# The third recurrent step of a gated graph network with its gates by nodes instead of by channels

## The chip, the cores and the metric

The kernel runs on one core of one Trainium2 chip. The metric is the device time of one execution in microseconds (us). The kernel before took 2534.15 us, the median of 3 runs (2533.99 to 2534.88).

A core has five engines, each with an instruction queue that it works through in order: TensorE (PE in the profile; its weight loads are listed as PEld), VectorE (DVE), ScalarE (ACT), GpSimd (POOL) and SyncE (SP), which here only issues transfers. They meet through semaphores. TensorE writes to PSUM, in banks of 128 partitions by 512 fp32 values; the other tiles of the kernel lie in SBUF.

## The reference, cut to what matters

64 graphs of 256 nodes with 256 channels, fp32, and an adjacency matrix of integers for each. Layer 0 is a gated graph network of three steps with shared gate weights, layer 1 a graph attention with four heads. Both have a normalization ahead and a residual around them.

```python
def _gru_cell(inp, h, w_ih, w_hh, b_ih, b_hh):
    gi = inp @ w_ih.T + b_ih
    gh = h @ w_hh.T + b_hh
    i_r, i_z, i_n = jnp.split(gi, 3, axis=-1)
    h_r, h_z, h_n = jnp.split(gh, 3, axis=-1)
    r = jax.nn.sigmoid(i_r + h_r)
    z = jax.nn.sigmoid(i_z + h_z)
    n = jnp.tanh(i_n + r * h_n)
    return (1.0 - z) * n + z * h

# layer 0
h = jnp.maximum(_layernorm(x), 0.0)
h0 = h
A = (adj != 0).astype(x.dtype)
for i in range(3):
    m = jnp.einsum('bnd,de->bne', h0, weight[i])
    aggr = jnp.einsum('bst,bsd->btd', A, m)
    h0 = _gru_cell(aggr, h0, w_ih, w_hh, b_ih, b_hh)
x = x + h0
# layer 1
h = jnp.maximum(_layernorm(x), 0.0)
x = x + gat(h, adj, W, b, a)      # four heads, masked softmax over the neighbours
```

## The kernel before, in words

Two graphs ("sequences" 0 and 1) make a pair; 32 pairs run one after the other, overlapped. Everything is planned in ticks: `at(tick, phase, p, fn)` puts a piece of work into a plan, and at the end the plan is emitted tick by tick, within a tick first the phase STEP, then READY, then REST, and within a phase the later pair first. That order of emission is the order on every engine's queue. A step of the recurrence takes six ticks (`SUB = 6`), the pairs start 18 ticks apart (`APART`), and pair p has its three steps at ticks 0 to 5, 12 to 17 and 24 to 29 of its own count. So exactly one step is in STEP at any time: the first step of pair p+1, the third of pair p, the second of pair p+1, and so on. Between them, in READY and REST, lie the normalizations, transposes, attention and transfers of the pairs around.

In all three steps the channels lie on the partitions: state hT, sums aggr, gates R and Z and the new value hn are tiles of 128 partitions by 2 channel halves by 512 (2 sequences of 256 nodes). `block` (L308, its matmuls at L312) makes one 256x256 product for one sequence: four matmuls with a 128x128 piece of a weight loaded and 256 nodes of the data moving. An fp32 matmul is two instructions in the profile, so a block is eight. `part` (L418) is one matmul with a 128x128 weight loaded; the three-products scheme for the state's share of the n gate has seven of them in a step: N00, NS1, NS2, N01, NS3, NS4, N11. They go into the banks qa and qb. Blocks are named by weights: RH, S1, S2, RA (gate r), RZ, S4, ZA (r of sequence 1, z), and NA once per sequence (input of gate n, banks pn0 and pn1).

The gate banks come from a ring of five (`ps_g`), the others from a ring of three (`ps_m`).

`tick_0` runs N00, copies qa to qb on ScalarE (L433), aggregates over the neighbours (L440, the copies to SBUF at L444), runs NS1 and copies m5n (L446). `tick_1` runs NS2; VectorE adds `q_b[:, N:] = q_b[:, :N] + m5n` (L453); block RH into pc; N01; ScalarE takes hn with its bias (`state_n`, L421) and copies pc to pd (L459); VectorE forms T3 and T2 (L461, L462). `tick_2` runs NS3 into `q_b[:, :N]`, which L453 has read, and NS4 into `q_b[:, N:]`, the last hn on VectorE (L468), block S1 with its copy m5 (L473), and T4 (L474). `tick_3` has S2 into pd, the sum into pe on VectorE (L479), RA and the first tanh (`tanh_half`, L425). `tick_4`: N11, `first_n(0)` ((R+1)·hn into pn0 on VectorE, L495), RZ, the sum for Z (L489), S4, tanh. `tick_5`: `first_n(1)`, NA of sequence 0 on top of pn0, ZA, NA of sequence 1, and `new_n` (tanh on ScalarE, L506, then the difference h − n on GpSimd, L510) for each. The biases are columns, one value per partition, and go in as the bias operand of ScalarE's activations, one instruction per channel half.

In READY of the tick behind a step, `update` (L527, L528 on VectorE) makes the new hT for both sequences. One and two ticks behind, `back` turns hT to nodes on partitions with four transposes per sequence (`turn_back`, L770): after steps one and two it takes from them the halves hNhi and hNlo for the next aggregation (L760, L761), after step three it adds them to x (`residual`, L776). x then goes through the second normalization (L339 to L351) and on to the attention. `divided` (L551, L553, L558) belongs to the attention's output of an earlier pair: VectorE divides a product (`po`, L542), GpSimd adds it to x. `maxima` (L899), the leaky relu (L919), the masks (L872) and the exponentials (L934) are also the attention's, each at ticks of its own.

The last pair's end is written out by hand in `plan_tail`: a tuple of pieces in the order in which they are emitted, sequence 0 ahead of sequence 1, with the leftover attention of the two pairs before in between.

Of the kernel before, what the change touches and what calls it, by code (L numbers as in the profile page):

```python
# [26 lines left out]
def gated_gnn_then_gat_kernel(  # L27
# [69 lines left out]
    def bank(name):  # L97
# [3 lines left out]
        "x": 5, "adj": 2, "edge": 2, "noedge": 2, "hT_a": 2, "xn": 2, "val": 2, "row": 4, "zz": 4, "o": 2,  # L101
# [44 lines left out]
    w_msgs += [load_square("row", f"w_msg_{l}", weight[l]) for l in range(1, L)]  # L146
# [39 lines left out]
    bhn = const.tile([P, KD], F32, name="bhn")  # L186

# [120 lines left out]
    def block(pt, w, j, src, start=False):  # L308

        for c in range(KD):  # L310
            for k in range(KD):
                nc.tensor.matmul(  # L312
                    pt[:, ts(c, N)], w[:, k, j * D + c * P : j * D + (c + 1) * P], src[:, k, :],
                    start=start and c == 0 and k == 0, stop=(c == KD - 1 and k == KD - 1),
                    skip_group_check=True,
                )

# [66 lines left out]
    class Step:  # L384


        def __init__(self, n_, l, hT, end):

            self.n_, self.l, self.hT, self.end = n_, l, hT, end
# [25 lines left out]


# [5 lines left out]

        def tanh_half(self, i, dst, src, g0):
            for c in range(KD):
                nc.scalar.activation(  # L425
                    of(dst, i)[:, c, :], src[:, c, :], AF.Tanh, bias=brz[:, g0 + c : g0 + c + 1], scale=0.5
                )

# [19 lines left out]
        def tick_1(self):  # L448
            h0 = of(self.hT(), 0)
            q_a, q_b = self.qa, self.qb  # L450
            self.own("hn", [P, KD, T])
            self.part(q_b[:, :N], NS2, self.T2n)
            nc.vector.tensor_add(q_b[:, N:], q_b[:, :N], self.m5n)  # L453
            p_c = self.bank("pc")
            block(p_c, w_h, RH, h0, start=True)
            self.part(q_a[:, :N], N01, h0[:, 1, :])
            self.state_n(0, 0, q_a[:, :N])
            self.bank("p5")
            nc.scalar.copy(self.bank("pd"), p_c)  # L459
            T3 = self.own("T3", [P, KD, N])  # L460
            nc.vector.tensor_sub(T3, of(self.aggr, 1), of(self.hT(), 1))  # L461
            nc.vector.tensor_add(self.own("T2", [P, KD, N]), T3, h0)  # L462

        def tick_2(self):
            q_b = self.qb
            self.part(q_b[:, :N], NS3, self.T3n)
            self.part(q_b[:, N:], NS4, of(self.hT(), 1)[:, 1, :])
            nc.vector.scalar_tensor_tensor(  # L468
                of(self.hn, 1)[:, 1, :], q_b[:, :N], bhn[:, 1:2], self.m5n, op0=ALU.add, op1=ALU.add
            )  # L470
            self.state_n(0, 1, q_b[:, N:])
            block(self.p5, w_a[self.l], S1, self.T1, start=True)
            nc.scalar.copy(self.own("m5", [P, T]), self.p5)  # L473
            nc.vector.tensor_sub(self.own("T4", [P, KD, N]), self.T2, of(self.aggr, 0))  # L474

        def tick_3(self):
            R_ = self.own("R", [P, KD, T])
            block(self.pd, w_a[self.l], S2, self.T2)
            nc.vector.tensor_add(self.bank("pe"), self.pd, self.m5)  # L479
            block(self.pc, w_a[self.l], RA, of(self.aggr, 0))  # L480
            self.tanh_half(0, R_, by_c(self.pc), 0)

        def tick_4(self):
            Z_ = self.own("Z", [P, KD, T])
            self.part(self.qb[:, :N], N11, self.T4n)
            self.state_n(1, 0, self.qb[:, :N])
            self.first_n(0)
            block(self.pd, w_h, RZ, self.T3)
            nc.vector.tensor_add(of(Z_, 1), by_c(self.pd), by_c(self.m5))  # L489
            block(self.pe, w_a[self.l], S4, of(self.aggr, 1))  # L490
            self.tanh_half(1, self.R, by_c(self.pe), 0)
# [7 lines left out]
        def input_n(self, i):  # L499
            block(getattr(self, f"pn{i}"), w_a[self.l], NA, of(self.aggr, i))  # L500

        def new_n(self, i):
            n__ = of(self.hn, i)
            p_n = by_c(getattr(self, f"pn{i}"))
            for c in range(KD):
                nc.scalar.activation(  # L506
                    n__[:, c, :], p_n[:, c, :], AF.Tanh, bias=bi[:, 2 * KD + c : 2 * KD + c + 1]
                )
            if not (self.end and i == 1):
                nc.gpsimd.tensor_sub(of(self.R, i), of(self.hT(), i), n__)  # L510

        def tick_5(self):
            self.first_n(1)
            self.input_n(0)
            self.tanh_half(1, self.Z, of(self.Z, 1), KD)
            block(self.pd, w_a[self.l], ZA, self.T4)
            self.new_n(0)
            self.tanh_half(0, self.Z, by_c(self.pd), KD)
            self.input_n(1)
            self.new_n(1)  # L520

        def update(self, i):

            d_ = of(self.R, i)
            if self.end and i == 1:
                nc.vector.tensor_sub(d_, of(self.hT(), i), of(self.hn, i))
            nc.vector.scalar_tensor_tensor(d_, of(self.Z, i), 1.0, d_, op0=ALU.add, op1=ALU.mult)  # L527
            nc.vector.scalar_tensor_tensor(of(self.hT(), i), d_, 0.5, of(self.hn, i), op0=ALU.mult, op1=ALU.add)  # L528

# [33 lines left out]
    def plan_tail(t0, p, v, g, turn_back, residual):  # L563


        val, zz, own, drow, mrow = None, {}, {}, {}, {}
# [22 lines left out]
        def result(i):  # L589
            if i == 0:  # L590
# [99 lines left out]
        def do(what, q, *key):  # L690
# [3 lines left out]
        order = (  # L694
            lambda: g.update(0), do("rows", 1), do("product", 2, 0), lambda: turn_back(0), lambda: g.update(1),
            do("product", 2, 1), lambda: residual(0), lambda: stats(0), do("add", 1), lambda: turn_back(1),
            do("product", 2, 2), lambda: residual(1), lambda: result(0), lambda: turned(0), lambda: stats(1),
            do("product", 2, 3), do("divided", 2, 0), lambda: values(0), lambda: result(1), lambda: turned(1),
            do("divided", 2, 1), do("divided", 2, 2), lambda: values_out(0), do("divided", 2, 3),
            do("write", 2), lambda: spread_scores(0), lambda: logits(0), lambda: leaky(0),  # L700
            lambda: values(1), lambda: values_out(1), lambda: maxima(0), do("exps", 1, 0), lambda: spread_scores(1),
            lambda: logits(1), lambda: leaky(1), lambda: spread_tops(0), do("product", 1, 0), do("product", 1, 1),
            lambda: maxima(1), lambda: spread_tops(1), do("exps", 1, 1), do("divided", 1, 0), do("divided", 1, 1),
            lambda: exps(0), do("product", 1, 2), do("product", 1, 3), lambda: exps(1), do("divided", 1, 2),
            do("divided", 1, 3), do("write", 1), lambda: output(0), lambda: output(1),
        )
        for k, fn in enumerate(order):
            at(t0 + SUB * (2 * L - 1) + 0.01 * (k + 1), READY, p, fn)

    def plan_pair(p):  # L710
# [40 lines left out]
        def back(l, i):  # L751

            def fn():
                if l < L - 1 and i == 0:
                    v["hN"] = node_halves(f"{p}_{l}")
                turn_back(l, i)
                pt = v["pback", i]
                hi, lo = (flat(y[:, i * KN : (i + 1) * KN, :]) for y in v["hN"])
                if l < L - 1:
                    nc.scalar.copy(hi, pt)  # L760
                    nc.vector.tensor_sub(lo, pt, hi)  # L761
                else:
                    residual(i)
            return fn

        def turn_back(l, i):
            pt = v["pback", i] = bank(f"pback_{p}_{l}_{i}")
            for s in range(KN):
                for k in range(KD):
                    nc.tensor.transpose(  # L770
                        pt[:, s * D + k * P : s * D + (k + 1) * P], h["hT"][:, k, ts(i * KN + s, P)], ident
                    )

        def residual(i):
            xi = flat(v["x"][:, i * KN : (i + 1) * KN, :])
            nc.vector.tensor_add(xi, v["pback", i], xi)  # L776

        for l in range(L):
            end = last and l == L - 1
            g = Step(f"{p}_{l}", l, lambda: h["hT"], end)  # L780
            t = 2 * SUB * l
            ready(t - 3 if l else t - 1, g.state_sums)
            ready(t + 2, g.last_state_sum)
            step(t, lambda g=g: g.tick_0(v["hN"], v["edge"]))
            for k, fn in enumerate((g.tick_1, g.tick_2, g.tick_3, g.tick_4, g.tick_5), 1):
                step(t + k, fn)
            if not end:
                ready(t + SUB, lambda g=g: g.update(0))
                ready(t + SUB, lambda g=g: g.update(1))
                for i in range(PB):  # L790
# [16 lines left out]
        if last:  # L807
            plan_tail(t0, p, v, g, lambda i: turn_back(L - 1, i), residual)
# [169 lines left out]
    at(2, REST, 0, load_vectors)  # L978
    at(5, REST, 0, lambda: step_weights_T(1))
# [38 lines left out]
```

## Time and profile before

| | |
|---|---|
| median of 3 runs | 2534.15 us |
| the profiled execution | 2540.86 us |
| its span, first to last instruction | 2539.1 us |
| mean granted TensorE clock | 0.995 |
| one period of the steady part (one pair) | 76.95 us |
| L312, blocks on TensorE, 6912 instructions | 13 to 20% of the chain of waits for each of pd, pn, pc |
| L418, parts on TensorE, 1344 instructions | 379 to 391 ns listed, by group |
| L770, transposes back, 768 instructions | 116.1 us busy |
| L776, residual additions on VectorE, 64 | 43.9 us busy, 685 ns each |
| L510, differences on GpSimd, 191 | 317.8 us busy, 1664 ns each |

The page lists for each engine the time in which at least one instruction was under way. TensorE's matmuls overlap, so a listed duration is longer than the distance from one start to the next; distances are read from the timeline. VectorE's and ScalarE's instructions overlap by less. A number in brackets behind a timeline line is the time that the engine stood idle before that instruction and what ended it.

### The profile page before, as it was taken

The page shows a single profiled execution, that of the slowest core. Times are in us where ns is not written, and L with a number is a line of the kernel's source. Part 1 is how long each engine was busy: PE and PEld are TensorE (multiplying, and loading weights), DVE is VectorE, ACT ScalarE, POOL GpSimd, SP SyncE. Part 2 cuts the span into 40 slices and gives each one's busy share as a digit, 9 for nine tenths or more (in the row PEclk, how much of TensorE's full clock was granted, in tenths as well). Part 3 has the DMA queues.
Part 4 walks back from the last instruction along what each step waited for, and adds up shares of the span by engine and source line. Part 5 has one row for each costly group of instructions (what it writes and reads, how often), then busy time and mean ns, then how long its engine had stood idle before and what let it go on. Part 6 is the DMA issues. An engine that isn't in the chain of part 4 may idle for free.

```text
span 2539.1 us, 38539 instructions
## 1 busy us (share of the span) xinstructions
PE 2514.5 (99%) x13918; PEld 2246.4 (88%) x13918; DVE 1824.1 (72%) x4458; ACT 1466.2 (58%) x3095; POOL 645.5 (25%) x514
## 2 busy tenths in 40 slices
PE   8999999999999999999999999999999999999998
PEld 6888898888889888989888988888988889898887
DVE  5567777677777777776777776777777777767667
ACT  3456565565555565555665655655656656556664
POOL 0122232222222222323232323222222223222221
PEclk9999999999999999999999999999999999999998
DMA  3033434553435544345544444534344544354443
GB/s 94 17 74 88 97 93 108 109 125 92 92 92 117 109 113 99 87 95 117 117 100 93 98 102 109 125 92 100 88 113 109 119 95 93 87 124 110 93 95 89
DMA packets 168223, 251.91 MB, mean 99 GB/s; under 512 B 42896, under 2 KB 128352, under 8 KB 168032
## 3 DMA queue, kind: packets, MB, share of 16 engines
q0 software_dynamic: 33728, 130.03, 26.6%
q1 hardware_dynamic: 132736, 119.41, 16.0%
q8 instruction: 110, 1.80, 0.3%
q14 instruction: 81, 0.66, 0.1%
q10 hardware_dynamic: 1568, 0.01, 0.0%
HBM read 215.62 MB, written 25.67 MB: 95 GB/s over the span
## 4 chain that ended last, share of the span: by engine, by line
PE 97%; DVE 1%; DMA 1%; ACT 1%; issue 0%; POOL 0%; SPq 0%; DVEq 0%
PE pd L312 20%; PE pn L312 13%; PE pc L312 13%; PE po L542 9%; PE pa L440 7%; PE qb L418 6%; PE pe L312 6%; PE p L312 6%; PE qa L418 5%; PE pv L820 4%; PE pback L770 3%; PE pt_a L370 1%; PE pt_b L370 1%; PE pc L238 1%; DVE any L899 0%; DMA hh_nat<-in_L_gnn_w_hh_dram 0%
## 5 line engine op out<-in xcount | busy, mean ns | idle before, releaser
L510 POOL TENSOR_TENSOR R<-hT_a,hn 128x512 f32<-128x512 f32 x191 | 317.8, 1664 | 879.4 <-ACT hn L506 821.5
L312 PE MATMUL pn<-aggr,w_a 128*128 128x256 f32 x1536 | 367.1, 382 | 0.0
L312 PE MATMUL pd<-T,w_a 128*128 128x256 f32 x1536 | 366.3, 381 | 0.0
L312 PEld LDWEIGHTS pn<-aggr,w_a 128*128 128x128 f32 x1536 | 287.0, 190 | 43.1 <-DVE pn L495 6.4
L312 PEld LDWEIGHTS pd<-T,w_a 128*128 128x128 f32 x1536 | 287.9, 191 | 37.6
L542 PEld LDWEIGHTS po<-val,zz 128*128 128x128 f32 x2048 | 250.3, 195 | 4.5
L542 PE MATMUL po<-val,zz 128*128 128x65 f32 x2048 | 247.2, 275 | 0.0
L899 DVE CUSTOM_DVE_ANT_0 any<-drow,noedge 128x256 f32<-128x256 f32 x496 | 236.9, 478 | 9.8 <-DMA drow<-score_dram 1.0
L506 ACT ACTIVATE hn<-pn,bi 128x256 f32<-128x256 f32 x384 | 160.3, 469 | 144.3 <-PE pn L312 144.2
L425 ACT ACTIVATE R<-pc,brz 128x256 f32<-128x256 f32 x192 | 80.5, 470 | 278.5 <-PE pc L312 278.5
L527 DVE SCALAR_TENSOR_TENSOR R<-Z,R 128x512 f32<-128x512 f32 x192 | 131.8, 687 | 147.6 <-POOL R L510 142.8
L558 POOL TENSOR_TENSOR x<-x,o 128x256 f32<-128x256 f32 x124 | 112.0, 904 | 481.6 <-DVE o L553 481.6
L761 DVE TENSOR_TENSOR hNlo<-pback,hNhi 128x512 fp32r<-128x512 f32 x128 | 88.4, 691 | 201.6 <-ACT hNhi L760 201.6
L919 ACT ACTIVATE zz<-zz,val 128x256 f32<-128x256 f32 x496 | 224.9, 509 | 0.0
L495 DVE SCALAR_TENSOR_TENSOR pn<-R,hn 128x512 f32<-128x512 f32 x192 | 142.5, 742 | 93.7 <-ACT hn L421 77.2
L425 ACT ACTIVATE R<-pe,brz 128x256 f32<-128x256 f32 x192 | 80.5, 470 | 185.9 <-PE pe L312 185.9
L528 DVE SCALAR_TENSOR_TENSOR hT_a<-R,hn 128x512 f32<-128x512 f32 x192 | 174.6, 909 | 14.3 <-ACT m5n L446 1.4
L312 PE MATMUL pd<-T,w_h 128*128 128x256 f32 x768 | 181.5, 379 | 0.0
L312 PE MATMUL pc<-aggr,w_a 128*128 128x256 f32 x768 | 181.5, 379 | 0.0
L312 PE MATMUL pe<-aggr,w_a 128*128 128x256 f32 x768 | 181.4, 379 | 0.0
L312 PE MATMUL pc<-hT_a,w_h 128*128 128x256 f32 x768 | 181.4, 379 | 0.0
L312 PE MATMUL p<-T,w_a 128*128 128x256 f32 x768 | 181.4, 379 | 0.0
(176 smaller groups left out, 5258.5 us busy)
## 6 DMA issues: line engine op xcount, KB each, us to landing
zz<-score_dram POOLq DMA_DIRECT2D x62, 1024.0 KB, 11.7
zz<-topT_dram POOLq DMA_DIRECT2D x62, 1024.0 KB, 8.7
adj<-in_adj_dram SPq DMA_DIRECT2D x64, 512.0 KB
drow<-score_dram SPq DMA_DIRECT2D x62, 512.0 KB
x<-in_x_dram SPq DMA_DIRECT2D x32, 512.0 KB
out_dram<-x SPq DMA_DIRECT2D x31, 512.0 KB
noedge_dram<-noedge SPq DMA_DIRECT2D x31, 256.0 KB
score_dram<-score SPq DMA_DIRECT2D x124, 4.0 KB
```

What stands on the lines that cost most here:

```text
L312: nc.tensor.matmul(pt[:, ts(c, N)], w[:, k, j * D + c * P : j * D + (c + 1) * P], src[:, k, :], start=start and c == 0 and k == 0, stop=(c ...
L418: nc.tensor.matmul(pt, w_n[:, j, :], src, start=start, stop=True, skip_group_check=True)
L425: nc.scalar.activation(of(dst, i)[:, c, :], src[:, c, :], AF.Tanh, bias=brz[:, g0 + c : g0 + c + 1], scale=0.5)
L440: nc.tensor.matmul(pt[:, ts(i, N)], hN[half][:, i * KN + s, ts(e, P)], edge[:, i * KN + s, :], start=(s == 0 and half == 0), stop=(s == KN ...
L495: nc.vector.scalar_tensor_tensor(by_c(self.bank(f"pn{i}")), of(self.R, i), 1.0, of(self.hn, i), op0=ALU.add, op1=ALU.mult)
L506: nc.scalar.activation(n__[:, c, :], p_n[:, c, :], AF.Tanh, bias=bi[:, 2 * KD + c : 2 * KD + c + 1])
L510: nc.gpsimd.tensor_sub(of(self.R, i), of(self.hT(), i), n__)
L527: nc.vector.scalar_tensor_tensor(d_, of(self.Z, i), 1.0, d_, op0=ALU.add, op1=ALU.mult)
L528: nc.vector.scalar_tensor_tensor(of(self.hT(), i), d_, 0.5, of(self.hn, i), op0=ALU.mult, op1=ALU.add)
L542: nc.tensor.matmul(po[:, ts(h_, VC)], zz[:, j, h_, ts(s, P)], v["val"][:, i * KN + j, ts(h_, VC)], start=(j == 0), stop=(j == KN - 1),)
L899: nc.vector.tensor_tensor_reduce(any_, drow[r // KN][:, h, :], v["noedge"][:, r, :], 1.0, -3.0e38, ALU.add, ALU.max, accum_out=v["top"][:, ...
L919: nc.scalar.activation(zz[:, h, :], zz[:, h, :], AF.Prelu, alpha=ALPHA, bias=v["val"][:, r, S0 + H + h : S0 + H + h + 1],)
```

## The change

Steps one and two of each pair stay as they are. The third step becomes a class of its own, `LastStep`, with nodes on the partitions for its gates: `block` and `part` load 128x128 pieces of the data and move the weights (256 columns in `block`, 128 in `part`). R, Z, hn and the new value come out by nodes, so the four transposes per sequence behind the step are gone, and `update` adds straight into x. As the biases now run along the free dimension, they are kept as rows that are the same on all partitions (`b_rows`, six row loads and four VectorE operations once); they are added on VectorE, or copied by ScalarE into a bank before the matmuls add to it. The update needs the state after step two by nodes: `back` of step two keeps a copy `h` of it.

```diff
-        "x": 5, "adj": 2, "edge": 2, "noedge": 2, "hT_a": 2, "xn": 2, "val": 2, "row": 4, "zz": 4, "o": 2,
+        "x": 5, "adj": 2, "edge": 2, "noedge": 2, "hT_a": 2, "xn": 2, "val": 2, "row": 2, "zz": 4, "o": 2,
...
-    w_msgs += [load_square("row", f"w_msg_{l}", weight[l]) for l in range(1, L)]
+    w_msgs += [load_square("noedge", f"w_msg_{l}", weight[l]) for l in range(1, L)]
...
+    def load_bias_rows():
+        for j, vector, g in ((BR, b_ih, 0), (BZ, b_ih, 1), (BI, b_ih, 2), (BH, b_hh, 2)):
+            nc.sync.dma_start(b_rows[:, j, :], on_all_rows(vector, g))
+        others = []
+        for g in range(2):
+            others.append(buf("o", [P, D], f"b_hh_{g}"))
+            nc.sync.dma_start(others[g], on_all_rows(b_hh, g))
+        at(9, READY, 0, lambda: bias_rows(others))
...
+    class LastStep(Step):
...
+        def block(self, pt, w, j, src, start=False):
+            for s in range(KN):
+                for k in range(KD):
+                    nc.tensor.matmul(
+                        pt[:, ts(s, D)], src[:, k, ts(s, P)], w[:, k, ts(j, D)],
+                        start=start and s == 0 and k == 0, stop=(s == KN - 1 and k == KD - 1),
+                        skip_group_check=True,
+                    )
+
+        def part(self, pt, j, src, start=False):
+            for s in range(KN):
+                nc.tensor.matmul(
+                    pt[:, ts(s, P)], src[:, ts(s, P)], w_n[:, j, :], start=start and s == 0, stop=True,
+                    skip_group_check=True,
+                )
...
+        def state_n(self, c, i, pt):
+            nc.vector.tensor_add(
+                self.mine(self.hn, i)[:, :, ts(c, P)], pt.rearrange("q (s n) -> q s n", s=KN), self.row(BH, c)
+            )
+
+        def last_state_n(self):
+            by_s = self.m5n.rearrange("q (s n) -> q s n", s=KN)
+            nc.vector.tensor_add(by_s, by_s, self.row(BH, 1))
+            nc.vector.tensor_add(
+                self.mine(self.hn, 1)[:, :, ts(1, P)], self.qb[:, :N].rearrange("q (s n) -> q s n", s=KN), by_s
+            )
+
+        def tanh_half(self, i, dst, src, g0):
+            nc.scalar.activation(self.mine(dst, i), src, AF.Tanh, scale=0.5)
+
+        def first_term(self):
+            return self.pc, False
+
+        def tick_0(self, hN, edge):
+            super().tick_0(hN, edge)
+            nc.scalar.copy(by_c(self.bank("pc")), self.row(BR))
...
+        def new_n(self, i, h):
+            hn_ = self.mine(self.hn, i)
+            p_n = by_c(getattr(self, f"pn{i}"))
+            nc.vector.tensor_add(p_n, p_n, hn_)
+            nc.scalar.activation(hn_, p_n, AF.Tanh)
+            if not (self.end and i == 1):
+                nc.gpsimd.tensor_sub(self.mine(self.R, i), self.nodes(h, i), hn_)
...
+        def tick_4(self):
...
+            self.first_n(0)
+            for i in range(PB):
+                nc.scalar.copy(by_c(self.bank(f"pn{i}")), self.row(BI))
+            self.block(self.pd, w_h, RZ, self.T3)
+            nc.vector.tensor_add(by_c(self.pd), by_c(self.pd), self.row(BZ))
+            nc.vector.tensor_add(self.mine(Z_, 1), by_c(self.pd), by_c(self.m5))
...
+        def tick_5(self, h):
+            self.first_n(1)
+            self.input_n(0)
+            self.input_n(1)
+            self.tanh_half(1, self.Z, self.mine(self.Z, 1), KD)
+            self.block(self.pd, w_a[self.l], ZA, self.T4)
+            self.new_n(0, h)
+
+        def tick_5_rest(self, h):
+            self.new_n(1, h)
+            self.tanh_half(0, self.Z, by_c(self.pd), KD)
+
+        def update(self, i, h, x_):
+            d_, n__, xi = self.mine(self.R, i), self.mine(self.hn, i), self.nodes(x_, i)
+            if self.end and i == 1:
+                nc.vector.tensor_sub(d_, self.nodes(h, i), n__)
+            nc.vector.tensor_add(xi, xi, n__)
+            nc.vector.scalar_tensor_tensor(d_, self.mine(self.Z, i), 1.0, d_, op0=ALU.add, op1=ALU.mult)
+            nc.vector.scalar_tensor_tensor(xi, d_, 0.5, xi, op0=ALU.mult, op1=ALU.add)
...
 # in back, behind step two
+                if l == L - 2:
+                    nc.scalar.copy(flat(v["h"][:, i * KN : (i + 1) * KN, :]), pt)
...
+            if final:
+                step(t + 5, lambda g=g: g.tick_5(v["h"]))
+                rest(t + 5, lambda g=g: g.tick_5_rest(v["h"]))
```

`tick_5_rest` stands in REST of its tick, behind the READY work; `update` stays in READY of the tick behind the step, now with an addition of x ahead of its two operations. In the last pair's hand-written order, sequence 1 now goes ahead of sequence 0, and the two `turn_back` and two `residual` pieces are gone.

## The prediction

> **What bounds the kernel now.** I read the page's busy shares and its chain of waits first, then the waits, then the timeline of the one period in which the changed step and the step behind it run, engine by engine.
>
> ```profile
> PE 2514.5 (99%) x13918; PEld 2246.4 (88%) x13918; DVE 1824.1 (72%) x4458; ACT 1466.2 (58%) x3095; POOL 645.5 (25%) x514
> ...
> PE 97%; DVE 1%; DMA 1%; ACT 1%; issue 0%; POOL 0%; SPq 0%; DVEq 0%
> ```
>
> TensorE sets the end. In the steady part the timeline repeats every 76.95 us (an aggregation starts at 1200.43, its successor at 1277.38), and 32 pairs of 76.95 make 2462 of the 2539.1 us span. TensorE hardly waits: the only wait on its path that recurs is 0.2 us of a weight load, 30 times. So a TensorE instruction removed is worth its spacing, and any new wait of TensorE costs all of it. The spacing is not the listed duration, since matmuls overlap: blocks of eight 256-column instructions start 1.73 us apart, 0.216 us each.
>
> The place that matters lies one tick behind the changed step, where the next pair's second step starts. These are the weight loads, VectorE and GpSimd of that place (start, duration, what it is):
>
> ```profile
> 1281.50 0.41 PEld L418 LDWEIGHTS qa<-hT_a,w_n 128*128 128x128 f32 x2
> 1281.93 0.57 PEld L770 LDWEIGHTS pback<-ident,hT_a 128*128 128x128 f32 x4
> 1282.47 0.30 PEld L418 LDWEIGHTS qb<-T3n,w_n 128*128 128x128 f32 x2
> ```
>
> ```profile
> 1276.93 0.18 DVE L551 RECIPROCAL rden<-po 128x4 f32<-128x4 f32 x1 [2.20 <-PE po L542]
> 1277.21 0.42 DVE L553 TENSOR_TENSOR o<-po,rden 128x256 f32<-128x256 f32 x1
> 1277.56 0.68 DVE L527 SCALAR_TENSOR_TENSOR R<-Z,R 128x512 f32<-128x512 f32 x1
> 1277.72 1.12 POOL L558 TENSOR_TENSOR x<-x,o 128x256 f32<-128x256 f32 x1 [0.34 <-DVE o L553]
> 1278.27 1.12 DVE L528 SCALAR_TENSOR_TENSOR hT_a<-R,hn 128x512 f32<-128x512 f32 x1
> 1279.31 0.68 DVE L527 SCALAR_TENSOR_TENSOR R<-Z,R 128x512 f32<-128x512 f32 x1
> 1280.09 0.69 DVE L528 SCALAR_TENSOR_TENSOR hT_a<-R,hn 128x512 f32<-128x512 f32 x1
> 1280.70 0.42 DVE L899 CUSTOM_DVE_ANT_0 any<-drow,noedge 128x256 f32<-128x256 f32 x1
> ...
> 1281.52 0.43 DVE L453 TENSOR_TENSOR qb<-qb,m5n 128x256 f32<-128x256 f32 x1
> ```
>
> VectorE stands still until a product of TensorE ends (1276.93), then runs without a gap to L453. The NS3 part of TensorE adds into what L453 reads, so it may not start before L453 ends at 1281.95; its load starts at 1282.47. The slack is 0.52 us, and 0.44 us of it is the four transposes in between (matmul starts 1282.14 to 1282.58), which the change removes.
>
> The second place is the changed step's own first tick: ScalarE and the load of block RH.
>
> ```profile
> 1250.39 1.07 ACT L444 COPY aggr<-pa 128x512 f32<-128x512 f32 x2
> 1251.34 0.40 ACT L446 COPY m5n<-qa 128x256 f32<-128x256 f32 x1
> 1251.60 1.09 ACT L934 ACTIVATE zz<-zz 128x1024 f32<-128x1024 f32 x1
> ```
>
> ```profile
> 1251.28 1.49 PEld L312 LDWEIGHTS pc<-hT_a,w_h 128*128 128x128 f32 x7
> ```
>
> RH is ready to start while ScalarE is still behind with the sums' copies.
>
> **The change, per pair.** *Transposes removed:* eight per pair, two fours of 0.44 us: −0.88.
>
> *Blocks:* still eight instructions of 256 columns; 0.
>
> *Parts:* seven per step, each now four instructions of 128 columns instead of two of 256. Before: two by 0.216 = 0.432. The nearest row is the spread of scores near the end, 128x128 against 128 columns: sixteen in 1.95 us, less the last one's 0.28, over 15, is 0.111 each, so 0.446 a part and +0.10 for seven. Bounds: 0.108, the transposes' spacing, gives 0; the other spread (2.02 us for sixteen) gives 0.116 and +0.24.
>
> *Bias row in pc:* RH no longer clears its bank but adds to a ScalarE copy of the bias row, put behind the copy of m5n. That copy can start at 1251.60, where the exponential starts now; the 128x512 copy of L459 takes 0.59, so 1252.19. RH's load wants to start at 1251.28, some 0.03 later by the longer parts: a wait of 0.91. Not all is lost: at 2456.07 the loads had waited 0.98 and the matmuls, due at 2455.25 (two of 0.227 behind 2454.80), 0.82; in shorter waits about 0.1 comes back too. I take +0.82; bounds 0.65 and 0.95. The exponentials queued behind the copy have two ticks of room.
>
> *Residual into update:* the two additions of L776 (0.685 each, in the ticks behind) go, two additions x+n of SBUF tiles (0.68, issued 0.60 apart like the neighbours here) come, but ahead of L453: +1.20 on that chain, against 0.08 of slack left.
>
> *Later input of the last difference:* VectorE now adds hn to pn before each tanh. The first addition waits for block NA of sequence 0, which ends near 1271.65, so first_n(1), this addition, the four normalizations (1.37) and two maxima (0.92) end near 1274.6, and GpSimd's first difference, in the midst of them, adds some 0.95 as it does now (the second maximum takes 1.37 instead of 0.42). The second addition then ends near 1276.3, its tanh near 1276.95, and GpSimd's second difference, 1.27 long, runs from 1277.0 to 1278.3, where now it is over at 1277.38. The first x+n, due at 1277.56, meets it. That neither runs through the other is read from L528 above: 1.12 instead of 0.69 beside a GpSimd addition. So +0.75 more on the chain.
>
> Sum for NS3: 1.20 + 0.75 − 0.08 + 0.05 to wake = 1.9 of wait; by the 0.1 to 0.2 that comes back, +1.75. Bounds: without the collision, and with the 0.43 that L528 loses now gone, 0.60; with GpSimd's next addition losing its turn into L527 too, 2.4. I take 1.75, since the first difference delays the maxima today and will again.
>
> The Trainium skill's "SBUF — State Buffer", section "Who interferes with whom", calls the port pair of VectorE and GpSimd an exclusive lock, which blocks a VectorE instruction with two SBUF inputs for the whole of a GpSimd instruction that reads SBUF. By it x+n would wait for the whole rest of the difference, 0.75; by the L528 row alone, which lost 0.43 beside a shorter operation, the pair would cost 0.3 less.
>
> *At nothing, with the cover:* ScalarE loses three hn copies, runs six whole tanhs for twelve halves, and gains three bias copies and two of h (0.58); those of h fall into its idle stretches of 2.04 and 3.68 us before the hn copy at 1233.05 and the tanh at 1239.23; uncovered they would be 1.2. VectorE waits for N01 in the changed step, with T3 and T2 queued behind; T2 then ends near 1256.2 and block S2 loads at 1259.5 even with RH late. Its three state additions and the split L468 (1.7) come before the addition into pe, which has RA, a product and N11 (3.9) to spare. The two additions on pd (1.38) end near 1268.4; ZA comes after both NA blocks at 1273.2. The bias copies into pn wait for the hn addition at 1265.8; NA needs them at 1269.8. TensorE waits at none of these; each is worth its overrun if VectorE is 2 us later than I count.
>
> *Once:* six row loads and their six SP issues (about 0.4 each, as L119) at tick 3, where the transfer queues are nearly empty; four VectorE operations (1.6) at tick 9, needed at tick 24. Two fewer "row" buffers: a pair's destination scores are fetched eight ticks behind the last maximum of the pair before. 0 to 2 us in all; I take 0.
>
> *The last pair:* its eight transposes ran in two groups at half clock (0.86 each between 2487.34 and 2492.36): −1.7, with +0.10 and +0.82: −0.8. The end can shift by some 4 us either way, since that half clock may come or go with the gap before it.
>
> **Sum.** −0.88 + 0.10 + 0.82 + 1.75 = +1.79 per pair, by 31 = +55.5, less 0.8: +54.7. On the profiled span of 2539.1 (2540.86 around it) that is 2593.8; the median of the runs lies 6.7 below the profiled execution, so 2534.15 + 54.7 = **2588.9**.
>
> **Rivals.** *(A) The forecast*, 50%: with 1.3 to 2.2 for NS3, 2575 to 2603. *(B) Only the added instructions delay L453*, 25%: the second difference is out of the way before 1277.5, NS3 costs 0.60 to 1.05, per pair +0.64 to +1.09: 2553 to 2567. For it: GpSimd is idle 75%. Against: the 1.37 us maximum. *(C) Only RH waits*, 5%: +0.04 per pair: 2535, no change; it needs L453 not to decide, against the 0.08 of slack. *(D) Faster*, 10%: the transposes come out whole and neither wait appears, −0.78 by 31 − 0.8: 2509. The mechanism is TensorE's 99% share; it decides if ScalarE's and VectorE's lateness together stay under 0.78 a pair. Against it: both line-by-line orders. *(E) The clock drops*, 10%: TensorE ran at half clock in two stretches:
>
> ```profile
> 94.00:96.00 2.00, 2.00 (x7) 1.63 (x7) 0.17 (x1) 0.00 (x0) 0.00 (x0) 0.53 0.00 0
> ...
> 2488.00:2496.00 8.00, 8.00 (x40) 8.00 (x39) 5.79 (x18) 2.97 (x8) 3.57 (x4) 0.50 0.29 58
> ```
>
> The granted clock (behind the five engines) fell after 1.94 us of idle within 4 us, and after 1.5 us at 2483.7. The first spell lasted some 3.4 us. A new wait of 1.9 us could do it each period: 1.7 more per pair, up to 2589 + 53 = 2642. Against: a 1.25 us gap at 53 did nothing. The Trainium skill's "TensorE: Matmul & The Clock Gate", section "Why this matters for your kernels", would put the limit at gaps of about 3 us; by it E never happens, by the 1.5 us row it can, and the row decides.
>
> Anything below 0.2% (5 us) I call no change. Faster 0.10 (D), same 0.05 (C), slower 0.85 (A, B, E). The range reaches from B's low end to a part of E: 2550 to 2620; A's own is 2575 to 2603.
>
> **What would show it.** In each period two waits of TensorE: RH for ScalarE's copy into pc (near 0.9) and the next step's NS3 for L453 (near 1.9, 0.7 under B); period 78.7 instead of 76.95; parts of four at 0.111; GpSimd's second difference overlapping the first x+n. Wrong would be: parts spaced above 0.13 (weight loads as the bound), no wait at RH, or a wait in a place that I put at nothing.

## The result, and the profile after

| | before | after |
|---|---|---|
| median of 4 runs each | 2534.52 us | 2594.69 us (2593.44 to 2595.51) |
| ratio to before, 95% interval | | 1.0235 (1.0218 to 1.0253) |
| span of the profiled execution | 2539.1 us | 2591.5 us |
| period of the steady part | 76.95 us | 78.65 us |
| TensorE busy | 2514.5 us, 99% | 2506.4 us, 97% |

The changed kernel is slower by 2.35%. The period grew by 1.70 us, and 31 of these are 52.7 us, where the spans differ by 52.4. The page's busy shares, then the shares of its chain of waits:

```profile
PE 2506.4 (97%) x14110; PEld 2236.1 (86%) x14110; DVE 1932.8 (75%) x4686; ACT 1463.8 (56%) x2967; POOL 636.0 (25%) x514
...
PE 84%; DVE 9%; ACT 5%; issue 2%; DMA 0%; DVEq 0%; POOL 0%; SPq 0%
```

TensorE's listed busy time falls by 8 us, as transposes went (by less than their spacing, since a part of each new wait lies inside listed durations); yet it holds only 84% of the chain instead of 97%, and VectorE and ScalarE have taken the rest. The waits of the weight loads say where (who waited for whom: us in total, times, longest):

```profile
PEld qb L446 <- DVE qb L490: 53.3, 31, 2.1
PEld pc L574 <- ACT pc L611: 25.3, 32, 0.8
PEld pn L437 <- DVE pn L530: 6.2, 29, 0.2
```

The third row is the wait that was there before. The first two are new and come once a pair: 1.72 us for L490 (L453 before), 0.79 us for the copy of the bias row. What a wait cost is read beside it, from where the matmuls start against where their spacing would have put them. The first place, the changed step's first tick, in the timelines of ScalarE, of the loads and of TensorE:

```profile
1198.83 0.40 ACT L483 COPY m5n<-qa 128x256 f32<-128x256 f32 x1
1199.09 0.62 ACT L611 COPY pc<-b_rows 128x512 f32<-128x512 f32 x1
```

```profile
1198.45 0.53 PEld L582 LDWEIGHTS qb<-w_n,T2n 128*128 128x128 f32 x4
1199.77 1.59 PEld L574 LDWEIGHTS pc<-w_h,hT_a 128*128 128x128 f32 x8 [0.79 <-ACT pc L611]
```

```profile
1198.56 0.61 PE L582 MATMUL qb<-w_n,T2n 128*128 128x128 f32 x4
1199.77 1.99 PE L574 MATMUL pc<-w_h,hT_a 128*128 128x256 f32 x8 [0.60 <-ACT pc L611]
1201.60 0.61 PE L582 MATMUL qa<-w_n,hT_a 128*128 128x128 f32 x4
...
1202.48 0.61 PE L582 MATMUL qb<-w_n,T3n 128*128 128x128 f32 x4
1202.93 0.61 PE L582 MATMUL qb<-w_n,hT_a 128*128 128x128 f32 x4
```

NS2 started at 1198.56; four instructions of 0.111 and RH's eight of 0.216 put N01 at 1200.73. It started at 1201.60: 0.87 lost. The last two rows are parts back to back, 0.45 apart (0.444 from the whole row of starts).

The second place, one tick behind the changed step: the loads, then GpSimd and VectorE:

```profile
1229.94 0.41 PEld L446 LDWEIGHTS qa<-hT_a,w_n 128*128 128x128 f32 x2
1232.10 0.30 PEld L446 LDWEIGHTS qb<-T3n,w_n 128*128 128x128 f32 x2 [1.75 <-DVE qb L490]
```

```profile
1225.24 1.29 POOL L623 TENSOR_TENSOR R<-h,hn 128x512 f32<-128x512 f32 x1 [2.28 <-ACT hn L621]
1226.49 1.19 POOL L690 TENSOR_TENSOR x<-x,o 128x256 f32<-128x256 f32 x1
```

```profile
1225.37 0.18 DVE L683 RECIPROCAL rden<-po 128x4 f32<-128x4 f32 x1 [0.83 <-PE po L674]
1225.66 0.42 DVE L685 TENSOR_TENSOR o<-po,rden 128x256 f32<-128x256 f32 x1
1226.00 1.09 DVE L658 TENSOR_TENSOR x<-x,hn 128x512 f32<-128x512 f32 x1
1227.01 1.22 DVE L659 SCALAR_TENSOR_TENSOR R<-Z,R 128x512 f32<-128x512 f32 x1
1228.26 0.69 DVE L660 SCALAR_TENSOR_TENSOR x<-R,x 128x512 f32<-128x512 f32 x1
1228.87 0.69 DVE L658 TENSOR_TENSOR x<-x,hn 128x512 f32<-128x512 f32 x1
1229.48 0.69 DVE L659 SCALAR_TENSOR_TENSOR R<-Z,R 128x512 f32<-128x512 f32 x1
1230.19 0.69 DVE L660 SCALAR_TENSOR_TENSOR x<-R,x 128x512 f32<-128x512 f32 x1
1230.81 0.42 DVE L1033 CUSTOM_DVE_ANT_0 any<-drow,noedge 128x256 f32<-128x256 f32 x1
...
1231.62 0.43 DVE L490 TENSOR_TENSOR qb<-qb,m5n 128x256 f32<-128x256 f32 x1
```

From the reciprocal's start to L490's end VectorE runs 6.68 us without a gap of more than 0.11; before, the same stretch (1276.93 to 1281.95) took 5.02. NS3 was due at 1230.59 (N01's start 1230.16 plus 0.43), NS4 therefore at 1231.03; NS4 started at 1232.63: 1.60 lost. So the period's sum as measured is −0.87 (transposes) + 0.08 (parts, 7 by 0.444 − 0.432) + 0.87 + 1.60 = +1.68, against 1.70 read.

The medians differ by 60.2 us and the profiles by 52.4, since a stretch of half clock near the end was in both profiled executions and, going by the mean granted clock (0.995 to 0.997), in the other three of after, but in only 10 of the 28 executions of before timed beside the experiments (0.994 to 0.996 with spans from 2537.9; the others 0.998 to 0.999, up to 2534.0). What a wait costs is therefore read from periods.

### The profile page after: what moved, and what is told of

The parts are those of the page before. It is cut to its first block, busy times and chain, and to the rows that moved or that the text cites. A ratio compares the mean times of both kernels' runs of the same rounds, so it can differ in the third digit from the quotient of the medians.

```text
span 2591.5 us, 39091 instructions
## 1 busy us (share of the span) xinstructions
PE 2506.4 (97%) x14110; PEld 2236.1 (86%) x14110; DVE 1932.8 (75%) x4686; ACT 1463.8 (56%) x2967; POOL 636.0 (25%) x514
## 4 chain that ended last, share of the span: by engine, by line
PE 84%; DVE 9%; ACT 5%; issue 2%; DMA 0%; DVEq 0%; POOL 0%; SPq 0%
PE pd L437 13%; PE pn L437 9%; PE po L674 9%; PE pc L437 6%; PE pd L574 6%; PE pc L574 4%; PE pe L437 4%; PE p L437 4%; PE pv L954 4%; PE qb L446 4%; PE pn L574 4%; PE pa L477 3%; DVE R L659 2%; PE p L574 2%; PE pback L893 2%; PE pe L574 2%
## 5 line engine op out<-in xcount | busy, mean ns | idle before, releaser
L544 POOL TENSOR_TENSOR R<-hT_a,hn 128x512 f32<-128x512 f32 x128 | 224.7, 1756 | 772.8 <-ACT hn L541 715.7
L437 PE MATMUL pn<-aggr,w_a 128*128 128x256 f32 x1024 | 244.4, 381 | 0.0
L437 PE MATMUL pd<-T,w_a 128*128 128x256 f32 x1024 | 243.0, 380 | 0.0
L437 PEld LDWEIGHTS pn<-aggr,w_a 128*128 128x128 f32 x1024 | 192.1, 190 | 31.2 <-DVE pn L530 6.2
L437 PEld LDWEIGHTS pd<-T,w_a 128*128 128x128 f32 x1024 | 192.6, 191 | 25.8
L477 PE MATMUL pa<-edge,hNhi 128*128 128x256 f32 x512 | 133.7, 299 | 0.0
L1006 ACT ACTIVATE zz<-link 128x1024 f32<-128x1024 bf16 x124 | 130.8, 1057 | 2.9 <-DMA link<-noedge_dram 2.9
L1068 ACT ACTIVATE zz<-zz 128x1024 f32<-128x1024 f32 x124 | 131.7, 1064 | 0.0
L481 ACT COPY aggr<-pa 128x512 f32<-128x512 f32 x192 | 106.9, 595 | 35.3 <-PE pa L477 35.3
L477 PE MATMUL pa<-edge,hNlo 128*128 128x256 f32 x512 | 125.4, 283 | 1.3 <-DVE hNlo L898 1.3
```

The source lines that it names most:

```text
L437: nc.tensor.matmul(pt[:, ts(c, N)], w[:, k, j * D + c * P : j * D + (c + 1) * P], src[:, k, :], start=start and c == 0 and k == 0, stop=(c ...
L477: nc.tensor.matmul(pt[:, ts(i, N)], hN[half][:, i * KN + s, ts(e, P)], edge[:, i * KN + s, :], start=(s == 0 and half == 0), stop=(s == KN ...
L481: nc.scalar.copy(aggr[:, e, :], pt)
L1006: nc.scalar.activation(logits[i][:, j, :, :], v["link"][:, j : j + 1, ts(i, N)].to_broadcast([P, H, N]), AF.Identity, scale=1 / 16,)
L1068: nc.scalar.activation(zz, zz, AF.Exp)
```

## The experiments

Losses per pair below come from the period: 76.95 before, and −0.79 for the transposes and the parts where the changed step is in. Three edits, each against one of the reasons, and the three together, came first.

**The row's copy earlier.** It is put ahead of the whole first tick, so RH should find it done.

```diff
         def tick_0(self, hN, edge):
+            nc.scalar.copy(by_c(self.bank("pc")), self.row(BR))
             super().tick_0(hN, edge)
-            nc.scalar.copy(by_c(self.bank("pc")), self.row(BR))
```

> The changed kernel, with ScalarE's copy of the bias row into pc put at the head of the step's first tick instead of behind the copy of m5n. My theory (RH waits for that copy): the 32 waits of RH, 25.3 us of its weight loads, go, and 0.87 us a pair comes back: 2594.7 - 28 = 2567 (2564 to 2571); the waits of NS3 stay at 53 us. Rival (RH is late for another reason, as weight loads of the state's pieces): no change, 2594.

Measured: 2581.78, ratio 1.0178 (1.0162 to 1.0194), period 78.26. RH's wait is gone, and another has come. The waits of the loads, then ScalarE:

```profile
PEld qb L446 <- DVE qb L490: 53.3, 31, 2.1
PEld qa L582 <- ACT qb L470: 15.3, 31, 0.9
```

```profile
1269.37 0.59 ACT L610 COPY pc<-b_rows 128x512 f32<-128x512 f32 x1
1269.89 0.34 ACT L470 COPY qb<-qa 128x256 f32<-128x256 f32 x1
```

ScalarE was behind already when the row's copy came up, so L470, which is queued behind it, slid; NS1 writes into the bank that L470 reads, and its load waited 0.48. Of the 0.87, only 0.39 came back (78.65 − 78.26), 13 us where 28 were expected. The wait was named rightly, the place for the copy was not.

**x + h instead of x + n.** With n + (Z+1)/2·(h − n) = h + (Z−1)/2·(h − n), h can be added to x well before the step ends, and `update` is back at two operations. The addition is put into `back` of step two, behind the copy of h.

```diff
                     nc.scalar.copy(flat(v["h"][:, i * KN : (i + 1) * KN, :]), pt)
+                    xi = flat(v["x"][:, i * KN : (i + 1) * KN, :])
+                    nc.vector.tensor_add(xi, pt, xi)
...
-            nc.vector.tensor_add(xi, xi, n__)
-            nc.vector.scalar_tensor_tensor(d_, self.mine(self.Z, i), 1.0, d_, op0=ALU.add, op1=ALU.mult)
+            nc.vector.scalar_tensor_tensor(d_, self.mine(self.Z, i), -1.0, d_, op0=ALU.add, op1=ALU.mult)
```

> The changed kernel, with x + h formed behind step two, where VectorE has room, so that update has again two operations per sequence. My theory (NS3 waits because two additions of 0.60 us stand ahead of L453): NS3's wait falls from 1.72 to 0.5 a pair, 31 x 1.2 = 37 us less: 2557 (2553 to 2565). Rival (the meeting of GpSimd's second difference with VectorE makes the wait): x - 1.0 us or less, 2585 to 2594.

Measured: 2587.97, ratio 1.0202 (1.0183 to 1.0221), period 78.23.

```profile
PEld pscore L972 <- PE pc L437: 30.7, 29, 1.1
PEld pc L574 <- ACT pc L611: 25.2, 32, 0.8
PEld qb L446 <- DVE qb L490: 13.5, 30, 1.5
```

NS3's wait fell from 1.72 to 0.45 (0.5 was expected), and a wait of 1.06 of the scores' transpose took its place. So the time lies in the range of the rival (2585 to 2594), but for another reason than the rival's. The releaser of the first row (an earlier matmul) does not say why; the waits of the matmuls themselves and the readers of pback do. First a row of the matmuls' waits, then who waited for an operation on pback (us, times):

```profile
PE pscore L972 <- DVE score L962: 21.8, 30, 1.9
```

```profile
  ACT h L899: 48.5, 64
  DVE x L901: 41.7, 64
```

The copy of h waits for VectorE's hNlo, x + h waits for the copy of h: three readers of one bank, one after another. In the kernel with all three edits the place in order of time is hNlo at 1248.57 for 0.70, the copy at 1249.29 for 0.59, x + h at 1249.91 for 0.69, and only then val at 1250.60. VectorE stands while ScalarE copies, and val, which the scores are taken from, is late. In the changed kernel the copy of h waits in the same way (48.5 us over 64), but there nothing stands behind it on VectorE.

The meeting with GpSimd, which this edit leaves in place, is still there. VectorE's two operations of the first sequence, where those of the second take 0.68 and 0.69:

```profile
1223.28 1.08 DVE L658 SCALAR_TENSOR_TENSOR R<-Z,R 128x512 f32<-128x512 f32 x1
1224.40 1.11 DVE L659 SCALAR_TENSOR_TENSOR x<-R,x 128x512 f32<-128x512 f32 x1
```

That is 0.81 lost, 0.38 more than the 0.43 of L528 before the change. It fits the 0.45 that NS3 still waits, but no run takes this meeting away by itself.

**The second difference earlier.** `new_n(1)` goes from REST to the end of the step's tick, so that GpSimd is done before x + n.

```diff
         def tick_5(self, h):
...
             self.new_n(0, h)
+            self.new_n(1, h)
 
         def tick_5_rest(self, h):
-            self.new_n(1, h)
```

> The changed kernel, with the last new value (VectorE's addition, tanh, GpSimd's difference) taken out of REST and put behind the first one, ahead of the normalization and the maxima. My theory: the second difference is over before x + n starts; the first x + n goes from 1.09 back to 0.69 us, 0.4 to 0.75 less per pair: 2571 to 2583. VectorE stands 1 us more behind the second input block, which its idle time ahead of the product (0.83) mostly holds. Rival (the collision is of no account, or VectorE's stand there costs as much): 2590 to 2600.

Measured: 2595.45, ratio 1.0230 (1.0214 to 1.0246), period 78.65: nothing. VectorE of this kernel:

```profile
1221.89 0.70 DVE L620 TENSOR_TENSOR pn<-pn,hn 128x512 f32<-128x512 f32 x1 [1.03 <-PE pn L574]
1222.50 2.54 DVE L362 TENSOR_SCALAR xn_a<-x,mv_a,rstd_a 128x256 f32<-128x256 f32 x4
...
1225.76 0.18 DVE L683 RECIPROCAL rden<-po 128x4 f32<-128x4 f32 x1
...
1226.39 0.68 DVE L658 TENSOR_TENSOR x<-x,hn 128x512 f32<-128x512 f32 x1
```

x + n takes 0.68 instead of 1.09: its collision is gone. But VectorE now waits 1.03 for block NA ahead of the normalization, and this now meets GpSimd's second difference, at 1223.30 to 1224.57 (2.54 for four; 2.32 in the changed kernel, where they meet the first difference alone). The idle 0.83 ahead of the reciprocal, which was the cover for such things, is used up: the reciprocal starts at 1225.76 instead of 1225.37, which takes back what x + n gained, and L490 is as late as it was. This is the rival's second half, that VectorE's stand costs as much.

**All three.**

> The three edits together. My theory: no wait of RH, NS3 waits 0 to 0.15; the eight transposes come out whole: 2534.5 - 31 x 0.75 - 2 = 2509 (2505 to 2517), below both kernels. Rival (each wait hides another behind it): 2530 or more.

Measured: 2573.70, ratio 1.0144 (1.0128 to 1.0159), period 77.85, where 2509 was expected. The new waits stay, as in the single edits: 1.06 for the transpose of the scores, 0.48 for NS1, and 0.49 for NS3. A remedy has to be looked at like the change itself: what is queued behind the moved instruction, and who reads the same bank.

**Is NS3's slack really nothing?** The reason says that in the kernel *before* any further VectorE work ahead of L453 is paid in full. One group of two maxima is put a tick earlier there; nothing else is changed.

```diff
-            ready(43 + y if not late else 45 + (3 * y) // 8, maxima(r, h0))
+            ready((43 + y if y != 6 else 48) if not late else 45 + (3 * y) // 8, maxima(r, h0))
```

> The kernel before, unchanged but for the attention's maxima: two of them (0.92 us on VectorE) move one tick earlier, so that they stand ahead of L453 in the step behind the third one. Nothing is added or left out, and the transposes stay. My theory (L453 had 0.52 us to spare before NS3): 0.40 of wait, some 0.3 of it lost, per pair: 2535 + 31 x 0.3 = 2544 (2540 to 2548), all of it as a wait of NS3 for L453. Rival (VectorE's order does not reach TensorE at this place): no change.

Measured: 2550.28, ratio 1.0054 (1.0037 to 1.0071), period 77.40.

```profile
PEld qb L418 <- DVE qb L453: 14.0, 30, 0.8
```

The load waits 0.47 on average, and 0.45 shows in the period; 0.40 of wait and 0.3 of loss were expected. So two maxima moved by one tick, with no work added, cost 14 us of span (31 by 0.45): this place decides in the kernel before too, and next to nothing of the wait came back here.

**Both remedies at better places.** The row's copy now stands behind the copy of qa (which NS1 waits for) and ahead of the sums' copies; x + h is a single addition of SBUF tiles, three ticks after `back` and in READY of a tick where VectorE has room.

```diff
             nc.scalar.copy(q_b[:, :N], q_a[:, :N])
+            self.first_row()
...
+        def x_plus_h():
+            nc.vector.tensor_add(flat(v["x"]), flat(v["x"]), flat(v["h"]))
+
+        ready(23, x_plus_h)
```

> The changed kernel with the row copy into pc between the copy of qb and those of the sums, and x + h formed from SBUF late in the tick in which VectorE waits for GpSimd. My theory: no wait of RH, of NS1 or of the score transpose, NS3 waits 0.45: per pair -0.87 + 0.08 + 0.4 = -0.4 against before: 2535 - 13 = 2522 (2517 to 2530). Rival (a copy or an addition only moves the wait, as the two first places for them did): over 2545.

Measured: 2527.44, ratio 0.9965 (0.9951 to 0.9978), period 76.44: 0.35% faster than before. One new wait is left, NS3's, 13.5 us over 30.

**And that one as well.** The maxima that stood ahead of L490 (from the sixth group on) are put one tick later.

```diff
-            ready(43 + y if not late else 45 + (3 * y) // 8, maxima(r, h0))
+            ready((43 + y if y < 5 else 44 + y) if not late else 45 + (3 * y) // 8, maxima(r, h0))
```

> The kernel of the run before, and the last three pairs of maxima one tick later, so that 0.92 us of VectorE go behind L453. My theory: NS3 does not wait at all and the transposes come out whole: 2535 - 31 x 0.79 - 1 = 2510 (2506 to 2518). Rival (the next wait behind it takes it): 2520 or more.

Measured: 2517.74 (2512.91 to 2521.08), ratio 0.9919 (0.9897 to 0.9942), period 76.16. Its longest recurring wait of a load, and one steady stretch (busy time of the five engines, with counts; then granted clock, transfers):

```profile
PEld pn L437 <- DVE pn L534: 6.1, 29, 0.2
```

```profile
1200.00:1278.00 78.00, 78.00 (x446) 70.35 (x445) 61.20 (x150) 45.61 (x93) 21.06 (x16) 1.00 0.45 102
```

Only the old wait of 0.2 is left and TensorE never stands. The period is 0.79 below before, which is the eight transposes (−0.87) and the parts (+0.08) to 0.01; 31 of them are 24.5, and the spans differ by 24.8. This version beats both kernels.

**The parts by themselves.** Three more runs put one edit alone on the changed kernel, to see whether the losses add up. First the maxima of the last run:

> The changed kernel with only those maxima one tick later. My theory (what stands ahead of L453 counts by its length, whatever it is): NS3's wait of 1.72 falls by 0.92: 2594.7 - 28 = 2566 (2563 to 2571). Rival (the additions of x, or the meeting with GpSimd, matter as such): less than 10 us.

Measured: 2567.97, ratio 1.0116 (1.0098 to 1.0133), period 77.83; NS3 waits 0.93 instead of 1.72, RH as ever. Then the row's copy behind qb's:

> The changed kernel with only the row copy into pc moved, between the copy of qb and those of the sums. My theory: RH waits for the copy and for nothing else, so 32 waits with 0.87 lost at each go and no wait of NS1 comes: 2594.7 - 28 = 2567 (2563 to 2571). Rival (some 0.4 us of ScalarE's work has to be late for TensorE wherever it lies, as with the copy at the head of the tick): 2578 or more.

Measured: 2564.03, ratio 1.0103 (1.0078 to 1.0127), period 77.77: 0.88 less than the changed kernel, all that RH had lost, with no new wait elsewhere. Last, x + h at tick 23:

> The changed kernel with only x + h formed from SBUF where VectorE waits for GpSimd. My theory: NS3's wait falls from 1.72 to 0.45, the loss from 1.60 to about 0.35, and nothing else waits: 2594.7 - 31 x 1.25 = 2556 (2552 to 2562). Rival (the additions' place is of no account, and the first try's gain was all that there is): 2580 or more.

Measured: 2554.21, ratio 1.0066 (1.0045 to 1.0087), period 77.30: 1.35 less. RH's wait stays (25.3 us over 32), NS3's is 0.44.

| changed kernel with | period | wait of RH | wait of NS3 | other new wait | period less 76.16 |
|---|---|---|---|---|---|
| nothing | 78.65 | 0.79 | 1.72 | | 2.49 |
| row's copy first of all | 78.26 | – | 1.72 | 0.48 (NS1) | 2.10 |
| row's copy behind qb's | 77.77 | – | 1.72 | | 1.61 |
| x + h in `back` | 78.23 | 0.79 | 0.45 | 1.06 (scores) | 2.07 |
| x + h at tick 23 | 77.30 | 0.79 | 0.44 | | 1.14 |
| maxima later | 77.83 | 0.79 | 0.93 | | 1.67 |
| row behind qb's, x + h at 23 | 76.44 | – | 0.45 | | 0.28 |
| these and maxima later | 76.16 | – | – | | 0 |

The last column is what all new waits cost together. The rows add up: 0.88 for the row's copy and 1.35 for x + h are 2.23, and the run with both gained 2.21.

## Why the prediction held, point by point

- **TensorE's spacing is the price of what goes and comes.** Right: transposes −0.87 (−0.88 said), parts +0.08 (+0.10 said, from the scores' spread; the upper bound there, four by 0.116, makes +0.22, not +0.24). The run without new waits shows the sum alone, −0.79 (−0.78 said).
- **RH waits for ScalarE's bias row.** Right in place and cause; +0.82 was said and 0.87 measured. The wait itself was read as 0.91 and is 0.79. The copy came when it was foreseen, 0.26 behind m5n's start, and took 0.62; but RH's load came up later. NS2's loads, now four, end 0.15 behind m5n's start (1198.98 against 1198.83), where RH's load before started 0.06 ahead of it (1251.28 against 1251.34). That some of the wait comes back was false here: RH lost more than its load waited. So 0.82 lies near 0.87 by two errors that nearly cancel.
- **NS3 waits for L453.** Right in place and cause, +1.75 said, 1.60 lost. The chain on VectorE grew by 1.66, where 1.95 was worked out. The two additions cost the 1.20. It is the *collision* that was mis-sized: 0.75 said. x + n lost 0.40 (1.09 for 0.69) and the operation behind it 0.53 to GpSimd's next addition, but before the change L528 lost 0.43 there, which went. Net 0.50, two thirds of it. The slack of 0.08 was misread too: 0.44, by the matmuls' starts, was taken from a slack that was read from the loads, and by the loads the transposes took 0.54 (1281.93 to 1282.47), so that nothing of the 0.52 was left. What came back, 0.12, fits the 0.1 to 0.2 said.
- **The second difference's time.** GpSimd's was foreseen for 1277.0 to 1278.3 in the old timeline, against a reciprocal at 1276.93; it came at 1225.24 to 1226.53, against a reciprocal at 1225.37. So 0.2 earlier, relative to it. The Trainium skill's "SBUF — State Buffer", section "Who interferes with whom", which makes VectorE's two-input operations wait for all of a GpSimd operation that reads SBUF, agrees to 0.13 us: x + n, listed from 1226.00, ended at 1227.09, 0.56 behind the difference's end at 1226.53, where that rule alone would make it 0.69. The operation behind it met GpSimd's next one in the same way: it ended at 1228.23, 0.55 behind that one's end at 1227.68.
- **What was put at nothing stayed at nothing.** No wait of a load but the two shows more than 0.2 per pair. The additions on pe, pd and pn, the copies of h and the row loads are all hidden.
- **Sum.** +1.79 per pair was said, +1.70 came. On the spans: 54.7 said, 52.4 measured; the last pair and what happens once are −0.3 of it, where −0.8 was said. The predicted median is lower than the measured one by 5.8 for another reason: 6.7 was taken off the profiled execution for the runs' median, as if the half clock at the end would be absent as often as before. By the mean clock it was there in all four runs.
- **Rivals.** *Only the added instructions* (2553 to 2567) needs no collision; the trace shows one. *Only RH waits* (2535) and *faster* (2509) fall with NS3's wait; the version with both waits removed then did what the faster rival says, by −0.79 a pair. *The clock drops each period* falls. Half clock came in more than the two stretches that the prediction names (0.50 from 16 to 18 us of the kernel before as well), but not in the steady part: one stretch over NS3's gap (1.35 us between TensorE's listed end and its next start) and one of the last pair:

```profile
1225.00:1237.00 12.00, 10.65 (x60) 9.32 (x60) 11.25 (x29) 7.32 (x17) 2.44 (x2) 1.00 0.26 89
```

```profile
2545.00:2550.00 5.00, 5.00 (x26) 5.00 (x25) 4.76 (x16) 0.51 (x2) 3.45 (x3) 0.50 0.22 39
```

The clock (behind the five engines) is full around the gap. A spell of half clock per period would have shown in the mean: 1.7 us lost of 78.65 is 0.978, and the mean granted clock is 0.997.

Not settled: how much of a load's wait is lost. NS3's came back by 0.12 to 0.17 in four kernels (1.72 for 1.60, 0.45 for 0.28, 0.44 for 0.27, 0.93 for 0.80), RH's (0.79 for 0.87) and that of the kernel before with its maxima moved (0.47 for 0.45) next to not at all.

## What to carry to other kernels

Removing work from the engine that sets the end is worth its spacing only if what replaces it does not come ahead of that engine's next operand; so follow each added instruction to the queue that it stands in and to the first wait behind it, with the slack in numbers. A remedy moves an instruction past others in turn, and is to be read in the same way: two of the three first ones here opened a wait of more than half of the one that they closed. Where a late operand can be exchanged for an early one by algebra (x + h for x + n), the gain alone (1.35) was larger than that of either change of order alone (0.88 and 0.82), provided that the early operand is read from a tile that nobody else is reading.

## What was not expected of the hardware

- A gap of TensorE of 1.35 us in each of 31 periods left the granted clock at 1.00 in the period shown and the mean at 0.997, while it fell to 0.50 for about 14 us behind a gap of 2.19 us near the end, in a stretch with other gaps.
- A 128-column fp32 instruction is 0.111 us behind the last one and a 256-column one 0.216: in this stream shorter instructions cost 3% more for the same columns, though twice as many weights are loaded.
- Three reads of one PSUM bank by two engines took their turns (0.70, 0.59, 0.69 us, each from the end of the last), each released by the one before as the trace has it. Whether the chip would let them overlap was not tried.
